# Linear attention between the tiles of a local-attention loop: residual fetched a stage ahead, an empty place behind five of its stages, output in three stages

## The chip, the cores and the metric

The kernel runs on one core of one Trainium2 chip. The time is the device time of one execution in microseconds. The time of a kernel is the median of several executions of the same program; the profile is one further execution, recorded instruction by instruction.

## The reference

Two blocks follow each other over `B = 2` sequences of `N = 2048` tokens with 128 features, all in float32. Each block adds a gated token mixer and a gated local-attention network to the residual `x`:

```python
h = layernorm(x) * (1 + ca) + sa;  x = x + ga * L0_attn(h)     # delta-rule attention
h = layernorm(x) * (1 + cb) + sb;  x = x + gb * L0_ffn(h)      # 6 layers of local attention, 16 heads, window 32
h = layernorm(x) * (1 + ca) + sa;  x = x + ga * L1_attn(h)     # causal linear attention and an MLP
h = layernorm(x) * (1 + cb) + sb;  x = x + gb * L1_ffn(h)      # 2 layers of local attention, 8 heads, window 64
```

The third line is the part that the change touches. Inside, it is

```python
xn = layernorm(x) * ln1_w + ln1_b
Q, K, V = elu(xn @ Wq.T + bq) + 1, elu(xn @ Wk.T + bk) + 1, xn @ Wv.T + bv
attn[t] = Q[t] @ sum_{s<=t} K[s] V[s]^T / (Q[t] . sum_{s<=t} K[s] + 1e-6)
x = x + attn @ Wo.T + bo
x = x + gelu((layernorm(x) * ln2_w + ln2_b) @ F1.T + b1) @ F2.T + b2
```

## The kernel before

After the delta-rule attention (about the first 600 us) all the rest is one long loop in `local_models`. It runs over the 8 layers of the two local-attention networks (6 and 2), over 16 tiles of 128 tokens, and over the 2 sequences: 256 tiles. The loop is a software pipeline. Iteration `i` does, in this order in the program: `scores` of tile i+1 (PE lines L982 and L991, then the softmax on DVE, ACT and POOL), `project` of tile i+3 (L871, in two halves in the 16-head layers), `keys_first_` of tile i (eight transposes, L1026), `values` of tile i+2 (L951, and eight or more copies of `v` by DMA from SyncE), `mix` of tile i (L1043), `turn` of tile i+2 (L923), `turn_out` (L1059) and `project_out` (L1071) of tile i.

Two lists of closures are worked off between these pieces. `steps` holds the six steps of a layer's feed-forward part for a block of 512 tokens (four tiles); `step()` runs one of them at two places of an iteration. `lsteps` holds the stages of the linear attention, and later those of the output; `lstep()` runs one of them, if there is one, at seven places of an iteration:

- place 1: at the top, ahead of `scores`
- place 2: after the first half of `project`
- place 3: after the second half of `project`
- place 4: after `keys_first_` and `values`
- place 5: after `mix` and `turn`
- place 6: after `turn_out`
- place 7: after the second `step()`, ahead of `project_out`

When the last step (`down`) of the sixth layer's feed-forward part is done for a block (b, k), it appends the stages of `linear(b, k)` to `lsteps`. There are 8 such blocks, two every eight iterations. The seventh layer projects its tiles from what these stages write into `hs0`, and calls `lstep()` in a loop if a block is not yet there. When `down` of the last layer is done, it appends `output(b, k)`.

One block of `linear` is a chain with hardly any parallelism: every stage hands on to another engine and gets the result back. `a0` fetches the residual `xb` from `xD` in HBM by DMA (L1247) and adds the gated branch to it on DVE (`outer`, L1187). Then come `centre` (PE L1096, squared on ACT L1098), `variance` (PE L1107, DVE L1112, POOL L1114), `a3` (PE transposes L1120, DVE L1123, ACT L1254 writes `h`), `centre` of `h`, `b2` to `b4` (PE L1263, DVE L1271 to L1282 write `z`, ACT exp), `c1` (PE transposes of `z`, L1291), `c2` to `c4`, `d1` (PE L1357, DVE L1359 writes `h` anew), `centre`, `variance`, `d4`, `e1` (PE L1370, Gelu on ACT), `e2` (PE L1381, DVE L1386 and L1388 write `xb`, which goes back to `xD`, L127), and `centre`, `variance` and `f3` for the next norm. Its buffers (pool `lw`) are single: the next block's `xb` can be fetched only when this block's store and its last `centre` are done.

The order in the program is not quite the order on the chip: the framework's scheduler sorts the instructions by readiness under a model of its own, with the program's order as the priority, and then every engine takes its own queue strictly in the resulting order. PSUM has two buffers of two banks (`wide`) and four of one bank (`bank`), which the loop and the linear stages share.

Of the kernel before, what the change touches and what calls it, by code (L numbers as in the profile page):

```python
# [11 lines left out]
F32 = mybir.dt.float32  # L12
# [8 lines left out]
NBLK = N // 512  # L21
# [51 lines left out]
def tile_kernel(ctx: ExitStack, tc: tile.TileContext, a: dict, out: bass.AP):  # L73
    nc = tc.nc
# [26 lines left out]
    def bc(ap, shape):  # L101
        return ap.to_broadcast(list(shape))
# [16 lines left out]
    xD = dram.tile([128, T], F32, name="xD")  # L119
# [588 lines left out]
    def local_models(mA, mB, hs0):  # L708
# [4 lines left out]
        lw = ctx2.enter_context(tc.tile_pool(name="l_w", bufs=1))  # L713
# [7 lines left out]
        def bank(name):  # L721
            return psT.tile([128, 512], F32, tag="T", name=f"ps_{name}")
# [371 lines left out]
        def centre(S, x, pool, keep):  # L1094
            p = bank("c")
            nc.tensor.matmul(p, lhsT=cen, rhs=x, start=True, stop=True)  # L1096
            S["sq"] = pool.tile([128, 512], F32, name="fsq")
            nc.scalar.activation(S["sq"], p, AF.Square)  # L1098
            if keep:
                S["xc"] = pool.tile([128, 512], F32, tag="t1", name="xc")  # L1100
                nc.scalar.copy(S["xc"], p)

        def variance(S, pool):
            p = bank("var")
            sq = S.pop("sq")
            for j in range(4):
                nc.tensor.matmul(  # L1107
                    p[:, j:j + 1], lhsT=sq[:, j * 128:(j + 1) * 128], rhs=onesm[:, 0:1],
                    start=True, stop=True,
                )  # L1110
            ve = pool.tile([128, 4], F32, name="fve")
            nc.vector.tensor_scalar(ve, p[:, 0:4], 1e-5, None, ALU.add)  # L1112
            S["rt"] = pool.tile([128, 4], F32, name="frt")
            nc.gpsimd.tensor_tensor(S["rt"], ve, bc(nhalf, (128, 4)), ALU.pow)  # L1114
# [11 lines left out]
        def feed_forward(g, b, blk):  # L1126
# [36 lines left out]
            def down():  # L1163
                p = bank("fy")
                for c, sz in enumerate(HSZ):
                    nc.tensor.matmul(  # L1166
                        p, lhsT=wts[g, "w2"][0:sz, c, :], rhs=S[c][0:sz],
                        start=(c == 0), stop=(c == 2),
                    )
                for lo, sh in ((0, 0), (64, 1)):  # L1170
                    cs = slice(n0 + sh, n0 + sh + 512)
                    nc.vector.scalar_tensor_tensor(
                        hs[0][lo:lo + 64, b, cs], p[lo:lo + 64, :], m.vec[lo:lo + 64, l, 8:9],
                        hs[1][lo:lo + 64, b, cs], ALU.add, ALU.add,
                    )
                if l == m.depth - 1:
                    lsteps.extend((linear if m is models[0] else output)(b, blk))
# [5 lines left out]
        def outer(b, k, gate, x):  # L1183

            n0 = k * 512
            for lo, sh in ((0, 0), (64, 1)):
                nc.vector.scalar_tensor_tensor(  # L1187
                    x[lo:lo + 64], hs0[lo:lo + 64, b, n0 + sh:n0 + sh + 512],
                    gate[lo:lo + 64, 5, b:b + 1], x[lo:lo + 64], ALU.mult, ALU.add,
                )  # L1190
# [48 lines left out]
        def linear(b, k):  # L1239
            S = {}  # L1240
            z = K["z"]
            vec = K["vec"]

            def a0():
                x = S["x"] = lw.tile([128, 512], F32, name="xb")
                blk = b * NBLK + k
                nc.sync.dma_start(x, xD[:, blk * 512:(blk + 1) * 512])  # L1247
                outer(b, k, mA, x)

            def a3():  # L1250
                xc = S.pop("xc")
# [140 lines left out]
            def f3():  # L1392
# [9 lines left out]
                ready.add((b, k))  # L1402

            return (
                a0, lambda: centre(S, S["x"], lw, True), lambda: variance(S, lw), a3,
                lambda: centre(S, S["h"], lw, False), b2, b3, b4, c1, c2, c3, c4, d1,
                lambda: centre(S, S["x1"], lw, False), lambda: variance(S, lw), d4, e1, e2,
                lambda: centre(S, S.pop("x"), lw, True), lambda: variance(S, lw), f3,
            )


        def output(b, k):
            S = {}
            blk = b * NBLK + k

            def residual():
                x = S["x"] = lw.tile([128, 512], F32, name="xb")
                nc.sync.dma_start(x, xD[:, blk * 512:(blk + 1) * 512])
                outer(b, k, mB, x)

            def leave():
                p = bank("out")
                x = S.pop("x")
                for c in range(4):
                    nc.tensor.transpose(
                        p[:, c * 128:(c + 1) * 128], x[:, c * 128:(c + 1) * 128], ident
                    )
                o = lw.tile([128, 4, D], F32, tag=f"t{1 + 2 * (k % 2) + b}", name="o")
                nc.scalar.copy(o.rearrange("p c d -> p (c d)"), p)
                nc.sync.dma_start(  # L1430
                    out[blk * 512:(blk + 1) * 512, :].rearrange("(c p) d -> p c d", p=128), o
                )

            return residual, leave


        models[0].consts()
# [9 lines left out]
        for i in range(-3, n):  # L1447
# [7 lines left out]
            if j < n:  # L1455
                g, b, t = tiles[j]
# [47 lines left out]
            if i >= 0:  # L1504
                g, b, t = tiles[i]
# [79 lines left out]
```

## Time and profile before

| | us |
|---|---|
| median of 3 runs | 5089.34 (5084.89 to 5097.49) |
| profiled execution | 5080.23 |
| its span | 5078.4 |
| PE busy | 4669.0 (92%) |
| DVE busy | 3876.9 (76%) |
| ACT busy | 2809.4 (55%) |
| POOL busy | 2760.7 (54%) |

PE is TensorE's matmuls, PEld its weight loads, DVE is VectorE, ACT is ScalarE, POOL is GpSimd, SP is SyncE, which issues the DMAs here. An instruction's idle time is the time that its engine stood still just before it, and the profile names what ended it. The mean granted clock of TensorE over the whole execution was 0.962 of full speed. By the times at which `project_out` of a layer's last tile ends, the fifth layer takes 2862.6 to 3420.6, the sixth 3420.6 to 4188.8, the seventh 4188.8 to 4661.0 us of the span. The linear attention's stages lie between about 3580 and 4360 us, in the sixth layer and at the start of the seventh. The output's stages lie in the last layer.

### The profile page before, as it was taken

The numbers are of one execution on the slowest core, as the hardware profiler recorded it, in microseconds if no ns is written. First come the engines' busy times: TensorE is split into PE (matmuls) and PEld (weight loads), VectorE is DVE, ScalarE is ACT, GpSimd is POOL, SyncE is SP. The second block draws the span as 40 slices with busy tenths as digits, with TensorE's granted clock in tenths as the row PEclk, the third lists the DMA queues.
The fourth block names the chain that finished last, engine by engine and source line by source line (L and its number), as shares of the span: only waits on it lengthen the run. The fifth ranks groups of instructions, "written<-read, shape, count | busy, mean of one in ns | idle before, by whom it ended". The sixth has DMA issues, their size and how long they took to land.

```text
span 5078.4 us, 171451 instructions
## 1 busy us (share of the span) xinstructions
PE 4669.0 (92%) x75012; PEld 3173.1 (62%) x75042; DVE 3876.9 (76%) x6760; ACT 2809.4 (55%) x4649; POOL 2760.7 (54%) x1650
## 2 busy tenths in 40 slices
PE   5657799999999999999999999999999988999998
PEld 4445566666666666666666666666666655566555
DVE  6993488787888788788887787787666656788886
ACT  3323356656656666565665566665555554565554
POOL 3332366566666666566666666666444433455553
PEclk8778899999999999999999999999999999999999
DMA  2000222232222222232222222232111111111121
GB/s 76 1 1 24 84 70 70 59 78 69 64 69 63 77 75 62 62 79 72 63 66 71 72 67 64 64 80 66 49 49 49 48 49 36 40 45 46 51 56 40
DMA packets 222490, 295.63 MB, mean 58 GB/s; under 512 B 75656, under 2 KB 95408, under 8 KB 221744
## 3 DMA queue, kind: packets, MB, share of 16 engines
q1 hardware_dynamic: 221744, 284.67, 21.7%
q8 instruction: 592, 9.70, 0.8%
q14 instruction: 154, 1.26, 0.1%
HBM read 40.98 MB, written 10.75 MB: 10 GB/s over the span
## 4 chain that ended last, share of the span: by engine, by line
PE 75%; DVE 6%; ACT 4%; issue 3%; POOL 2%; DMA 0%; SPq 0%; ACTq 0%; POOLq 0%; DVEq 0%
PE ps_qk L871 15%; PE ps_y L1071 8%; PE ps_turn L923 8%; PE ps_o L1043 7%; PE ps_s L991 7%; PE ps_v L951 6%; PE ps_f L1141 6%; PE ps_oT L1059 4%; PE ps_pT L1026 3%; PE ps_fy L1166 3%; PE ps_c L1096 1%; PE ps_var L1107 1%; PE ps_s L982 1%; ACT sq L873 1%; DVE t L886 1%
## 5 line engine op out<-in xcount | busy, mean ns | idle before, releaser
L892 POOL TENSOR_TENSOR r<-r,t 128x1024 f32<-128x1024 f32 x448 | 1059.6, 2365 | 1151.8 <-DVE t L886 1071.1
L873 ACT ACTIVATE sq<-ps_qk 128x1024 f32<-128x1024 f32 x448 | 459.3, 1025 | 1305.8 <-PE ps_qk L871 1299.7
L904 POOL TENSOR_TENSOR r<-r,rq_y 128x1024 f32<-128x1024 f32 x448 | 844.6, 1903 | 252.1 <-DVE rq_y L180 251.3
L871 PE MATMUL ps_qk<-wp,hs 128*128 128x512 f32 x1792 | 876.4, 611 | 32.8 <-DVE rq_y L180 18.8
L886 DVE TENSOR_TENSOR t<-ps_qk,tb 128x1024 f32<-128x1024 f32 (+1 forms) x512 | 553.4, 1081 | 178.8 <-POOL r L892 178.8
L1017 POOL TENSOR_TENSOR sm<-sm,rs 128x1024 f32<-128x1024 f32 x256 | 489.3, 1912 | 272.8 <-DVE rs L1016 161.4
L881 DVE TENSOR_TENSOR r<-ps_qk,tb 128x1024 f32<-128x1024 f32 (+1 forms) x512 | 548.9, 1072 | 103.3 <-ACT sq L873 101.7
L897 DVE TENSOR_REDUCE ps_qk<-sq 128x16 f32<-128x1024 f32 x448 | 549.7, 1227 | 13.5
L871 PEld LDWEIGHTS ps_qk<-wp,hs 128*128 128x128 f32 x1792 | 310.0, 190 | 351.2 <-issue 257.0
L1071 PEld LDWEIGHTS ps_y<-oT,wo 128*128 128x128 f32 x3584 | 438.5, 192 | 119.0 <-issue 73.4
L1071 PE MATMUL ps_y<-oT,wo 128*128 128x128 f32 x3584 | 481.1, 282 | 17.0 <-ACT oT L1060 16.4
L923 PE MATMUL ps_turn<-ident,r 128*128 128x128 f32 x3584 | 472.5, 282 | 26.0 <-issue 15.5
L1043 PEld LDWEIGHTS ps_o<-v,pT 64*32 64x32 f32 (+1 forms) x26624 | 344.1, 109 | 232.4 <-ACT pT L1027 109.2
L999 DVE TENSOR_REDUCE mx<-ps_s 128x16 f32<-128x1024 f32 (+1 forms) x256 | 313.1, 1223 | 186.7 <-PE ps_s L991 182.5
L951 PE MATMUL ps_v<-wp,hs 128*128 128x512 f32 x896 | 445.8, 597 | 2.1 <-DVE xc L1123 1.6
L923 PEld LDWEIGHTS ps_turn<-ident,r 128*128 128x128 f32 x3584 | 396.3, 143 | 57.8 <-issue 17.7
L1043 PE MATMUL ps_o<-v,pT 64*32 64x64 f32 (+1 forms) x26624 | 392.9, 224 | 37.2 <-issue 19.0
L991 PE MATMUL ps_s<-kT,qT 64*32 64x64 f32 (+1 forms) x26624 | 404.7, 230 | 4.6 <-ACT kT L928 4.1
L991 PEld LDWEIGHTS ps_s<-kT,qT 64*32 64x32 f32 (+1 forms) x26624 | 331.7, 107 | 79.6 <-issue 44.1
L1141 PE MATMUL ps_f<-fx,w 128*128 128x512 f32 (+1 forms) x768 | 364.7, 599 | 1.7 <-DVE fx L1123 1.7
L1049 ACT COPY on<-ps_o 128x512 f32<-128x512 f32 x448 | 244.6, 590 | 215.2 <-PE ps_o L1043 215.0
L1026 PEld LDWEIGHTS ps_pT<-ident,sm 128*128 128x128 f32 x2048 | 244.0, 142 | 145.7 <-issue 142.6
(266 smaller groups left out, 7661.9 us busy)
## 6 DMA issues: line engine op xcount, KB each, us to landing
v<-vn SPq DMA_DIRECT2D x1276, 128.0 KB
v<-vn SPq DMA_DIRECT2D x744, 64.0 KB
v<-vn SPq DMA_DIRECT2D x64, 256.0 KB
wp<-in_L_ffn_Wqkv SPq DMA_DIRECT2D x20, 512.0 KB
xD<-xb SPq DMA_DIRECT2D x24, 256.0 KB
xb<-xD SPq DMA_DIRECT2D x24, 256.0 KB
cs<-in_cos SPq DMA_DIRECT2D x128, 32.0 KB
cs<-in_sin SPq DMA_DIRECT2D x128, 32.0 KB
```

The lines of the kernel that those rows point to most:

```text
L871: nc.tensor.matmul(pq[:, js], lhsT=hw, rhs=wts[g, u][:, js], start=True, stop=True)
L881: nc.vector.tensor_tensor(r[:, es].rearrange("p (h d) -> p h d", d=DH), pq[:, es].rearrange("p (h d) -> p h d", d=DH), bc(tb[:, 0, s].unsq ...
L886: nc.vector.tensor_tensor(t2[:, es].rearrange("p (h s d) -> p h s d", s=2, d=32), pq[:, es].rearrange("p (h s d) -> p h s d", s=2, d=32)[: ...
L892: nc.gpsimd.tensor_tensor(r, r, t2, ALU.add)
L897: nc.vector.tensor_reduce(pq[:, 16 * v:16 * v + 16], st[i].pop(("sq", v)).rearrange("p (h d) -> p h d", d=DH), AX.X, ALU.add,)
L904: nc.gpsimd.tensor_tensor(rv, rv, bc(y[:, 16 * v:16 * v + 16].unsqueeze(2), (128, 16, DH)), ALU.mult)
L923: nc.tensor.transpose(p[:, c * 128:(c + 1) * 128], r[:, cs], ident)
L951: nc.tensor.matmul(p, lhsT=hw, rhs=wv, start=True, stop=True)
L991: nc.tensor.matmul(sp[W * w:W * w + W, c0:c0 + 2 * W], lhsT=qT[64 * q:64 * q + 64, cc, W * w:W * w + W], rhs=kT[64 * q:64 * q + 64, cc, W ...
L1043: nc.tensor.matmul(po[s][W * w:W * w + W, co:co + 64], lhsT=pT[kp, q, c, W * w:W * w + W], rhs=v2[kp, w, co:co + 64], start=True, stop=True,)
L1071: nc.tensor.matmul(py[:, 0:128], lhsT=wts[g, "o"][:, c * NO + s, :], rhs=oT[:, s, c, :], start=(c + s == 0), stop=(c == 3 and s == NO - 1),)
L1141: nc.tensor.matmul(ps_[c][0:sz], lhsT=wts[g, "w1"][:, o:o + sz], rhs=S["x"], start=True, stop=True,)
```

## The change

`linear` gets 27 stages in place of 21. The DMA of the residual leaves `a0` and becomes a stage of its own, `fetch`, with an empty stage between it and `a0`; further empty stages (`rest`, which does nothing) stand behind `a3`, `b4`, `d1` and `e2`. An empty stage takes one of the seven places of an iteration. `output` gets three stages in place of two: `fetch`, `residual`, `leave`. No arithmetic changes, nor do buffers or the number of instructions that compute.

```diff
@@ linear
+            def fetch():
+                blk = b * NBLK + k
+                S["x"] = lw.tile([128, 512], F32, name="xb")
+                nc.sync.dma_start(S["x"], xD[:, blk * 512:(blk + 1) * 512])
+
             def a0():
-                x = S["x"] = lw.tile([128, 512], F32, name="xb")
-                blk = b * NBLK + k
-                nc.sync.dma_start(x, xD[:, blk * 512:(blk + 1) * 512])
-                outer(b, k, mA, x)
+                outer(b, k, mA, S["x"])
+
+            def rest():
+                pass
...
             return (
-                a0, lambda: centre(S, S["x"], lw, True), lambda: variance(S, lw), a3,
-                lambda: centre(S, S["h"], lw, False), b2, b3, b4, c1, c2, c3, c4, d1,
-                lambda: centre(S, S["x1"], lw, False), lambda: variance(S, lw), d4, e1, e2,
-                lambda: centre(S, S.pop("x"), lw, True), lambda: variance(S, lw), f3,
+                fetch, rest, a0, lambda: centre(S, S["x"], lw, True), lambda: variance(S, lw), a3,
+                rest, lambda: centre(S, S["h"], lw, False), b2, b3, b4, rest, c1, c2, c3, c4, d1,
+                rest, lambda: centre(S, S["x1"], lw, False), lambda: variance(S, lw), d4, e1, e2,
+                rest, lambda: centre(S, S.pop("x"), lw, True), lambda: variance(S, lw), f3,
             )
@@ output
+            def fetch():
+                S["x"] = lw.tile([128, 512], F32, name="xb")
+                nc.sync.dma_start(S["x"], xD[:, blk * 512:(blk + 1) * 512])
+
             def residual():
-                x = S["x"] = lw.tile([128, 512], F32, name="xb")
-                nc.sync.dma_start(x, xD[:, blk * 512:(blk + 1) * 512])
-                outer(b, k, mB, x)
+                outer(b, k, mB, S["x"])
...
-            return residual, leave
+            return fetch, residual, leave
```

## The prediction

> **What bounds the kernel now.** I read the page first, then busy time by layer, then PE's waits in the stretch with the linear attention, then the timeline at single waits.
>
> ```profile
> span 5078.4 us, 171451 instructions
> PE 4669.0 (92%) x75012; PEld 3173.1 (62%) x75042; DVE 3876.9 (76%) x6760; ACT 2809.4 (55%) x4649; POOL 2760.7 (54%) x1650
> ```
>
> PE is the bound. The windows of the fifth, sixth and seventh layer (columns: us, busy of PE, PEld, DVE, ACT, POOL, granted clock, DMA share, GB/s):
>
> ```profile
> 2862.60:3420.60 558.00, 547.33 (x10450) 377.27 (x10448) 451.33 (x736) 341.31 (x561) 354.03 (x207) 0.99 0.27 68
> 3420.60:4188.80 768.20, 708.16 (x10850) 475.92 (x10848) 516.77 (x914) 415.84 (x660) 366.06 (x222) 0.96 0.20 52
> 4188.80:4661.00 472.20, 436.99 (x3717) 279.39 (x3716) 354.88 (x757) 258.23 (x407) 223.16 (x145) 0.97 0.15 42
> ```
>
> The fifth layer leaves PE idle for 10.7 us, the sixth for 60, the seventh for 35, and in these two the granted clock is lower. The waits of PE from 3565 to 4340 us (us in total, times, longest):
>
> ```profile
> PE ps_c L1096 <- ACT h L1254: 11.7, 4, 3.3
> PE ps_qk L1291 <- DVE z L1282: 10.1, 6, 3.5
> PE ps_c L1096 <- DVE xb L1388: 5.7, 3, 3.7
> PE ps_c L1096 <- DVE h L1359: 5.1, 4, 2.4
> PE ps_c L1096 <- ACT pT L1027: 4.7, 3, 2.5
> PE ps_r L1120 <- POOL frt L1114: 4.2, 7, 0.9
> ...
> PE ps_c L1096 <- issue: 2.7, 1, 2.7
> ...
> PE ps_c L1096 <- DVE xb L1187: 2.3, 1, 2.3
> ...
> PE ps_c L1096 <- PE ps_s L991: 1.9, 2, 1.0
> ```
>
> Nearly all of PE's idle time here is one linear stage waiting for the one before. The first, second, third and fourth row are the links behind `a3`, `b4`, `e2` and `d1`, where the change puts a rest; the L1096 rows with pT, issue, L1187 and ps_s (11.6 us) are the centre of `xb` behind `a0`. Together 44.2 us.
>
> One such wait in PE's timeline, and windows around it and around another (at 3737.39, 2.35 us idle):
>
> ```profile
> 3601.60 2.08 PE L1096 MATMUL ps_c<-h,cen 128*128 128x512 f32 x2 [3.34 <-ACT h L1254]
> ```
>
> ```profile
> 3593.90:3600.70 6.80, 4.36 (x20) 2.28 (x18) 5.54 (x8) 3.52 (x6) 4.21 (x3) 1.00 0.00 1
> 3600.70:3607.50 6.80, 5.90 (x138) 4.23 (x139) 4.04 (x11) 3.03 (x5) 5.44 (x6) 0.50 0.10 22
> 3737.30:3740.70 3.40, 3.31 (x90) 1.84 (x91) 3.19 (x8) 0.60 (x1) 2.19 (x1) 0.50 0.02 5
> ```
>
> After the wait the clock is 0.50 for 3.4 or 6.8 us: the two matmuls took 2.08 us, where those of ps_c<-hs, after no wait, have a mean of 614 ns each. From 3565 to 4340 us the clock record has 15 such stretches; 11 begin at one of the waits above. Matmul starts within those 11 lie 18.5 us further apart in sum than the medians of the same lines.
>
> **The change part by part.** It adds and removes no computing instruction; it moves stages. What counts is how much other PE work stands between a stage and the next. PE's work per 16-head tile, from the groups' busy time over 256 or 192 tiles: scores 2.35, each half of project 1.96, pT 1.13, values 1.99, mix 1.89, turn 2.11, turn_out 1.11, project_out 2.15. So between places 1 and 2 lie 4.3 us, 2-3 2.0, 3-4 3.1, 4-5 4.0, 5-6 1.1, 6-7 a feed-forward step or nothing, 7-1 2.15. Before, a block has 21 = 3 x 7 stages and always starts at place 7. After, 27 stages: first blocks of a pair start at 7, second blocks at 6. The cover of each link in us:
>
> | link | before | after, first block | after, second block |
> |---|---|---|---|
> | a0 to centre | 2.15 | 2.0 | 4.3 |
> | a3 to centre of h | 3.1 | 1.1 + step | 5.1 |
> | b4 to c1 | 2.15 | 7.1 | 5.1 |
> | d1 to centre | 1.1 | 5.1 | 6.3 |
> | e2 to centre | 3.1 | 6.3 | 6.4 |
>
> The need is the cover before plus the mean wait per block: a0 3.6, a3 4.6, b4 3.4, d1 1.7, e2 3.8. So:
>
> - **d1 and e2**: covered in all blocks. Gain 10.8.
> - **b4**: covered while the tiles are 16-headed. Around the change to the seventh layer they become 8-headed and an iteration takes about 11 us instead of 16.6; in the built order the first block there has only values, mix, turn and turn_out between `b2` and `c1`. The two waits over 3 us before (3.18 and 3.54) belong to blocks around this change; I keep both, 6.7. Gain 3.4.
> - **a3**: second blocks are covered. First blocks get turn_out and, in three of four, three matmuls of the feed-forward gate (L1141, half of 364.7 us over 64 blocks: 2.85). Left: 3.5 once, 0.6 three times: 5.3. Gain 6.4.
> - **a0**: 2.0 in program order is short, but the built order puts `outer` earlier on DVE or the centre behind turn_out in most blocks. I leave 2. Gain 9.6.
>
> Gaps gained: 30.2 us. Of the 11 half-clock stretches (1.7 us each) I leave three, at the three waits over 2.3 us that I leave: gain 13.5.
>
> [...]
>
> **The fetch.** In the built order of both kernels the DMA stands as early as the single `xb` buffer allows. DVE waited for it five times in the kernel, 9.2 us in all, and only 2.3 us of PE's waits name the instruction behind; these are counted at a0. What changes is that blocks now follow each other at once: 54 places of 56 per pair instead of 42. The chain store, landing, fetch, landing took from 3667.87 (end of L1388) to 3675.12 (start of L1187), 7.25 us; from `e2` to `a0` there are now 7 places, a whole iteration of 16.6 or 11 us, so no wait is added. On SP the fetch waits for the store (12.3 us, six times) with the copies of `v` queued behind; those themselves waited 153.5 us for `mix` to free their buffer, so they have room. If that cover went, `mix` would wait: at most 3.3 us a block.
>
> **Output.** PE waited 1.0 us ahead of ps_out (L1425) in each of six blocks before the tail. `leave` moves from behind project_out (place 1) to behind scores and projection (place 2): gain 5 of 6. In the tail the order of instructions is the same.
>
> **New waits.** The stages meet other work: variance to transposes is now often filled with mix and turn while POOL is at its 2.4-us additions; `h2` frees a PSUM bank that turn needs. Nothing in the trace shows them. From below 0; from above see the first rival. The nearest rows are the short waits there now (0.5 to 0.9 us, L1120); I take 1 us a block: 8.
>
> Sum: 30.2 + 13.5 + 5 - 8 = 40.7. From the profiled 5080.2 that is 5039.5; the median of the runs stands 9.1 above the profiled execution, so 5089.3 - 40.7 = 5048.6. I say 5049.
>
> **Rivals.**
> - **Two wide PSUM buffers (slower).** `u`, `kv` and `num` each hold one of two wide buffers until DVE has read them; scores and projection need both. In first blocks `b2` now stands at place 1 and `b3` at 2, with scores and a projection between; in the built order the second half of project slips behind the first matmuls of mix. From the start of `u` to its last read took 4.2 us in the first block before (3609.26 to 3613.48); with a half-clock stretch 5.9. For: PE takes its queue in order. Against: the same tiles cross projections before, and such waits (L871 on DVE sm) came to 3.0 us. It decides when 24 tiles cost over 40.7 + 8 us, 2.0 each; at 3.0 each (72): 5089 - 48.7 + 72 = 5112. Chance 0.12.
> - **Given back (same).** The waits close but the queues of DVE, ACT and POOL, which now carry linear and feed-forward work in every iteration, make the loop wait elsewhere: 4 to 5 us a block, 5 x 8 = 40. For: in the seventh layer DVE is busy 75% beside PE's 93%. Against: in the fifth layer PE is at 98% with DVE at 81%. 5089. Chance 0.14.
> - **The seventh layer takes more of the work and keeps its waits**: gain halved, 5069, still faster. Chance 0.2.
> - The forecast: 0.54.
>
> A measurement of this kernel can tell about 0.3% (15 us) from no change. Faster 0.54 + 0.2 = 0.74, same 0.14, slower 0.12. The low end: every widened wait and its clock gone and no new ones, 44.2 + 18.5 + 5 = 67.7, less the 6.7 around the seventh layer: 5028. The high end takes in the case of no gain: 5092; what lies above is most of the first rival.
>
> **What would show it.** Right: the rows L1096 on h, on xb and on L1359's h, and L1291 on z, fall from 44.2 to some 14 us; the clock of the sixth layer rises from 0.96 to 0.98; the layer gets shorter by some 25 us and the seventh by 10; L1425's idle goes. Wrong: L871 or L982 waiting for z, rq_y or rd (first rival); PE's idle as large as before under other names (second); L1187 waiting for its DMA in all blocks.

## The result, and the profile after

| | before | after |
|---|---|---|
| median, us | 5086.24 (5074.44 to 5097.49, 6 runs) | 5043.47 (5038.07 to 5053.27, 6 runs) |
| ratio | | 0.9923, 95% interval 0.9909 to 0.9937 |
| profiled execution, us | 5080.23 | 5053.27 |

The kernel became faster by 42.8 us, where the prediction had 40.7. The experiments will show that the sum came out so near with a wrong picture of the places behind it, and the terms, measured one by one, do not add up to it. The profiled execution of after is the slowest of its six runs, so the two profiles differ by only 27.0 us.

**A correction comes first.** The text above gives an iteration of the loop seven places for `lstep()`. The printed code has six calls: there is none between `turn_out` and the second `step()`. The places are:

- place 1: at the top, ahead of `scores`
- place 2: after the first half of `project`
- place 3: after the first `step()` and the second half of `project`
- place 4: after `keys_first_` and `values`
- place 5: after `mix` and `turn`
- place 6: after `turn_out` and the second `step()`

This number is used from here on. The prediction's covers, its starting places, and its "54 places of 56" are all wrong. Eight iterations have 48 places. A pair of 21-stage blocks takes 42 of them; a pair of 27-stage blocks takes 54, so each pair slides one iteration further. The traces agree: from the first `ps_c<-xb` of one pair to that of the next took 212.5 us before (3586.3 to 3798.8, eight iterations) and 224.4 us after (3592.4 to 3816.8, nine). And since 27 is 21 plus one whole iteration, blocks start at places 6 and 3 in both kernels.

The page of after:

```profile
span 5051.4 us, 171478 instructions
PE 4682.5 (93%) x75042; PEld 3190.3 (63%) x75042; DVE 3883.5 (77%) x6760; ACT 2796.3 (55%) x4645; POOL 2761.1 (55%) x1650
```

PE is busy no less than before (13.5 us more in the profile); the span shrank because PE stands idle less. The windows of the fifth, sixth and seventh layer of after (columns as before):

```profile
2867.10:3423.10 556.00, 545.53 (x10450) 375.45 (x10448) 451.08 (x736) 340.73 (x561) 353.92 (x207) 1.00 0.27 69
3423.10:4138.40 715.30, 680.39 (x10730) 466.73 (x10728) 514.18 (x885) 400.37 (x645) 363.10 (x218) 0.97 0.21 55
4138.40:4635.10 496.70, 459.61 (x3837) 297.17 (x3836) 365.30 (x786) 263.33 (x418) 227.48 (x149) 0.97 0.15 41
```

The sixth layer is 52.9 us shorter and the seventh 24.5 us longer. PE's idle time fell from 60 to 34.9 us in the sixth and is 37.1 us in the seventh (35.2 before): part of the linear work has slid into the seventh layer, and its waits with it. (These bounds of the layers, here and in the text above, stand one tile late in both kernels. At the true ends, 3403.8, 4163.0 and 4649.4 us before and 3406.4, 4118.8 and 4623.5 after, the sixth layer is 46.8 us shorter and the seventh 18.3 us longer.)

PE's waits in the linear stretch of after (us in total, times, longest), and the groups of the two lines that matter:

```profile
PE ps_r L1120 <- POOL frt L1114: 17.1, 9, 3.6
PE ps_aT L1355 <- DVE at L1347: 6.5, 3, 3.0
PE ps_o L1043 <- ACT pT L1027: 4.9, 5, 2.8
PE ps_qk L1296 <- DVE ps_qk L178: 3.1, 1, 3.1
...
PE ps_qk L1296 <- DVE z L1287: 1.7, 2, 1.3
```

```profile
L1096 PE MATMUL ps_c<-h,cen 128*128 128x512 f32 x30 | 16.3, 626 | 0.0
L1096 PE MATMUL ps_c<-xb,cen 128*128 128x512 f32 x30 | 15.6, 602 | 0.0
L1120 PE MATMUL ps_r<-ident,frt 128*128 128x128 f32 x124 | 20.4, 296 | 17.1 <-POOL frt L1114 17.1
```

Not one row of L1096 is left: the rests closed the links behind `a0`, `a3`, `d1` and `e2` completely. What took part of their place is L1120, the transposes of the reciprocal root of the variance: 4.2 us before, 17.1 now, and 21.6 when the late blocks up to 4480 us are counted too.

### The profile page after: what moved, and what is told of

It reads as the page before. It is cut to its first block, busy times and chain, and to the rows that moved or that the text cites. A ratio compares the mean times of both kernels' runs of the same rounds, so it can differ in the third digit from the quotient of the medians.

```text
span 5051.4 us, 171478 instructions
## 1 busy us (share of the span) xinstructions
PE 4682.5 (93%) x75042; PEld 3190.3 (63%) x75042; DVE 3883.5 (77%) x6760; ACT 2796.3 (55%) x4645; POOL 2761.1 (55%) x1650
## 4 chain that ended last, share of the span: by engine, by line
PE 75%; DVE 6%; ACT 4%; issue 2%; POOL 2%; DMA 0%; SPq 0%; ACTq 0%; POOLq 0%; DVEq 0%
PE ps_qk L871 15%; PE ps_y L1071 8%; PE ps_turn L923 8%; PE ps_o L1043 7%; PE ps_s L991 7%; PE ps_v L951 6%; PE ps_f L1141 6%; PE ps_oT L1059 4%; PE ps_pT L1026 4%; PE ps_fy L1166 3%; PE ps_var L1107 1%; PE ps_c L1096 1%; PE ps_s L982 1%; POOL r L892 1%; ACT sq L873 1%
## 5 line engine op out<-in xcount | busy, mean ns | idle before, releaser
L892 POOL TENSOR_TENSOR r<-r,t 128x1024 f32<-128x1024 f32 x448 | 1059.9, 2366 | 1162.4 <-DVE t L886 1075.2
L886 DVE TENSOR_TENSOR t<-ps_qk,tb 128x1024 f32<-128x1024 f32 (+1 forms) x512 | 552.8, 1080 | 180.5 <-POOL r L892 180.4
L881 DVE TENSOR_TENSOR r<-ps_qk,tb 128x1024 f32<-128x1024 f32 (+1 forms) x512 | 547.7, 1070 | 103.1 <-ACT sq L873 102.1
L897 DVE TENSOR_REDUCE ps_qk<-sq 128x16 f32<-128x1024 f32 x448 | 549.6, 1227 | 13.5
L1071 PE MATMUL ps_y<-oT,wo 128*128 128x128 f32 x3584 | 482.8, 282 | 18.7 <-ACT oT L1060 18.2
L923 PE MATMUL ps_turn<-ident,r 128*128 128x128 f32 x3584 | 470.6, 281 | 22.9 <-issue 12.0
L923 PEld LDWEIGHTS ps_turn<-ident,r 128*128 128x128 f32 x3584 | 395.2, 143 | 54.4 <-issue 15.8
L991 PEld LDWEIGHTS ps_s<-kT,qT 64*32 64x32 f32 (+1 forms) x26624 | 330.1, 107 | 70.3 <-issue 37.3
```

Source lines behind the costliest of these rows:

```text
L881: nc.vector.tensor_tensor(r[:, es].rearrange("p (h d) -> p h d", d=DH), pq[:, es].rearrange("p (h d) -> p h d", d=DH), bc(tb[:, 0, s].unsq ...
L886: nc.vector.tensor_tensor(t2[:, es].rearrange("p (h s d) -> p h s d", s=2, d=32), pq[:, es].rearrange("p (h s d) -> p h s d", s=2, d=32)[: ...
L892: nc.gpsimd.tensor_tensor(r, r, t2, ALU.add)
L897: nc.vector.tensor_reduce(pq[:, 16 * v:16 * v + 16], st[i].pop(("sq", v)).rearrange("p (h d) -> p h d", d=DH), AX.X, ALU.add,)
L923: nc.tensor.transpose(p[:, c * 128:(c + 1) * 128], r[:, cs], ident)
L991: nc.tensor.matmul(sp[W * w:W * w + W, c0:c0 + 2 * W], lhsT=qT[64 * q:64 * q + 64, cc, W * w:W * w + W], rhs=kT[64 * q:64 * q + 64, cc, W ...
```

## The experiments

Each experiment was timed in five rounds against before. For every profile I summed two things in the stretch from 3500 to 4480 us: PE's idle time (gaps over 0.05 us), and the extra time of matmuls under the half clock (start-to-start distances over the medians of the same pairs of lines at full clock). The idle time is sorted by the PE instruction behind it. "Five links" are those behind `a0`, `a3`, `b4`, `d1` and `e2`; "variance" is the wait for `frt`, the reciprocal root, ahead of the transposes (L1120) of `a3`, `d4` and `f3`.

| kernel | stages | idle | of it: five links | variance | half-clock extra | idle + extra, against before | profile from the sixth layer on | median against before |
|---|---|---|---|---|---|---|---|---|
| before | 21 | 84.4 | 50.0 | 4.2 | 31.4 | | | |
| after | 27 | 61.5 | 5.7 | 21.6 | 31.8 | -22.5 | -29.5 | -42.8 |
| e1_rests | 25 | 94.6 | 12.9 | 33.2 | 33.9 | +12.7 | +16.0 | +17.1 |
| e2_fetch | 23 | 96.1 | 13.6 | 44.1 | 36.2 | +16.5 | +16.9 | +20.1 |
| e3_output | 21 | 83.8 | 50.0 | 4.3 | 32.6 | +0.6 | -2.2 | 0.0 |
| e4_lump | 27 | 71.6 | 23.6 | 13.7 | 11.6 | -32.6 | -32.5 | -32.8 |
| e5_rests_dve | 25 | 102.1 | 13.8 | 41.1 | 23.4 | +9.7 | +13.5 | +19.1 |
| e6_after_dve | 27 | 68.7 | 17.8 | 13.2 | 18.7 | -28.4 | -31.4 | -28.8 |
| e7_lump7 | 28 | 78.0 | 19.1 | 15.2 | 36.6 | -1.2 | +2.1 | -0.1 |
| e8_rest_var | 27 | 54.2 | 6.2 | 6.8 | 31.3 | -30.3 | -32.6 | -32.0 |
| e9_var_at_3 | 27 | 79.9 | 7.6 | 30.7 | 36.9 | +1.0 | +4.1 | +1.6 |
| e10_best27 | 27 | 81.5 | 19.8 | 12.5 | 43.3 | +9.0 | +10.2 | -1.4 |
| e11_33stages | 33 | 66.5 | 12.7 | 9.2 | 37.3 | -12.0 | -15.3 | -19.0 |
| e12_second_later | 21, second blocks 27 | 82.8 | 30.5 | 18.9 | 42.9 | +9.9 | +9.1 | +8.6 |

Idle time and half-clock time together account for the profiled difference to within 4 us in every experiment (7 us in after). So the profiles are read from these two. The medians need not differ by as much as single profiles do: after gains 29.5 us by its profile and 42.8 by the medians.

### The parts of the change one at a time

**e1_rests**: the four rests alone, with 25 stages; fetch and output as before.

```diff
-a0, centre, variance, a3, centre, b2, b3, b4, c1, ... d1, centre, ... e2, centre, variance, f3
+a0, centre, variance, a3, rest, centre, b2, b3, b4, rest, c1, ... d1, rest, centre, ... e2, rest, centre, variance, f3
```

> Only the four empty stages behind a3, b4, d1 and e2 are added (25 stages); the residual is fetched in a0 and the output has two stages, as before. Theory 1 (the gain comes from the closed waits between two linear stages on PE): most of the gain is here, 20 to 35 us, and the waits of L1096 on h and on L1388's xb and of L1291 on z fall by more than half; the centre behind a0 keeps some of its 11.6 us. Theory 2 (the earlier fetch brings the gain): no change. Theory 3 (the gain comes from linear work that slides into the seventh layer, whose PE has more free time, 7% against 2%): four of six added places, so two thirds of the gain, some 28 us, with the waits unchanged.

**e2_fetch**: the stages `fetch` and the first `rest` alone, 23 stages.

```diff
-a0, centre, variance, a3, ...
+fetch, rest, a0, centre, variance, a3, ...
```

> Only the residual's fetch is a stage of its own with one empty stage behind it (23 stages); no other empty stage, output as before. Theory 1: a3 to centre of h now has 1.1 us of cover in first blocks and 2.15 in second ones against a need of 4.6, so what a0 gains is lost there: from 8 us faster to 8 us slower. Theory 2: the whole gain, some 40 us. Theory 3: two of six places, 14 us faster.

**e3_output**: only `output` in three stages; `linear` as before.

> Only the output has three stages; linear as before. Theory 1 as predicted: the six idle times of 1.0 us ahead of ps_out go, 5 us faster; by the profile after, where the last layer got only 1 us shorter, 0 to 2 us, which these runs can't tell from none. Theories 2 and 3: no change.

**e4_lump**: the 21 stages unbroken, with the six empty places in a lump behind `f3`.

```diff
-..., centre, variance, f3
+..., centre, variance, f3, rest, rest, rest, rest, rest, rest
```

> Linear keeps its 21 stages in unbroken order, and six empty stages stand behind f3 (27 in all, as many as after the change); residual fetched in a0, output as before. The same delay and the same slide into the seventh layer, without any spacing. Theory 1: no gain, rather 5 to 20 us slower, since second blocks now start at place 6, where a0 to centre, and b4 to c1, have no matmuls between them. Theory 3: the whole gain, some 40 us faster. Theory 2: no change.

Measured: e1_rests 5098.27, ratio 1.0031 (1.0019 to 1.0043); e2_fetch 5101.24, ratio 1.0041 (1.0028 to 1.0054); e3_output 5081.19, ratio 1.0000 (0.9989 to 1.0011); e4_lump 5048.36, ratio 0.9934 (0.9919 to 0.9949); before 5081.18.

So two parts of the change, each alone, make the kernel slower, and a version that spaces nothing gains 33 us. Neither the rests nor the early fetch brings the gain alone, and a gain of this size needs no spacing. Theory 3 (sliding) had the gain of e4_lump about right, but had 28 us for e1_rests and 14 for e2_fetch. The waits of e1_rests, e2_fetch and e4_lump, one row each:

```profile
PE ps_r L1120 <- POOL frt L1114: 32.7, 14, 5.9
```

```profile
PE ps_r L1120 <- POOL frt L1114: 44.1, 18, 6.0
```

```profile
PE ps_r L1120 <- POOL frt L1114: 13.6, 9, 4.7
```

The rests of e1_rests do close their links (50.0 to 12.9 us in the table), but the wait for `frt` takes back 29.0 us and other waits 18.3 us. What makes that wait is seen in the timeline of e2_fetch, in its second block:

```profile
3684.58 1.02 PE L1096 MATMUL ps_c<-xb,cen 128*128 128x512 f32 x2
3687.29 1.05 PE L1107 MATMUL ps_var<-onesm,fsq 128*128 128x1 f32 x8
3688.11 1.21 DVE L886 TENSOR_TENSOR t<-ps_qk,tb 128x1024 f32<-128x1024 f32 x1
...
3689.11 1.88 PE L951 MATMUL ps_v<-wp,hs 128*128 128x512 f32 x4
3689.24 0.24 DVE L1016 RECIPROCAL rs<-rs 128x16 f32<-128x16 f32 x1
3689.40 1.16 DVE L881 TENSOR_TENSOR r<-ps_qk,tb 128x1024 f32<-128x1024 f32 x1
3689.47 2.35 POOL L892 TENSOR_TENSOR r<-r,t 128x1024 f32<-128x1024 f32 x1 [6.43 <-DVE t L886]
...
3691.78 1.90 POOL L1017 TENSOR_TENSOR sm<-sm,rs 128x1024 f32<-128x1024 f32 x1
3691.85 1.22 DVE L886 TENSOR_TENSOR t<-ps_qk,tb 128x1024 f32<-128x1024 f32 x1 [1.29 <-POOL r L892]
3692.99 0.15 DVE L1112 TENSOR_SCALAR fve<-ps_var 128x4 f32<-128x4 f32 x1
...
3693.64 2.34 POOL L892 TENSOR_TENSOR r<-r,t 128x1024 f32<-128x1024 f32 x1
3695.94 1.01 POOL L1114 TENSOR_TENSOR frt<-fve,nhalf 128x4 f32<-128x4 f32 x1
...
3697.01 1.12 PE L1120 MATMUL ps_r<-ident,frt 128*128 128x128 f32 x4 [6.02 <-POOL frt L1114]
```

The variance matmuls end at 3688.3. Their consumer on DVE takes 0.15 us, but it stands behind the rotary products of the projection just done and starts at 3692.99; one of those (L886) waits 1.29 us for POOL's L892. The `pow` on POOL takes 1.0 us, but stands behind another 2.34 us of L892. PE has only `keys_first_` and `values` to do meanwhile and then stands still for 6.02 us. This is a variance at place 3, right behind the projection. In e2_fetch second blocks start at place 5, which puts the variance of `x` and that of `x1` at place 3: 6.0, 6.0, 4.2, 3.1 and 3.5, 3.6, 1.5, 2.8 us in the four blocks, 30.7 of its 44.1. Before and after have no variance at place 3.

e3_output shows that the third stage gains nothing. PE's waits in the last layer, first of before, then of e3_output:

```profile
PE ps_o L1043 <- ACT pT L1027: 6.1, 11, 0.7
PE ps_out L1425 <- issue: 3.0, 3, 1.0
PE ps_out L1425 <- DVE xb L1187: 2.1, 2, 1.0
```

```profile
PE ps_o L1043 <- ACT pT L1027: 8.1, 11, 1.7
PE ps_v L951 <- ACT o L1431: 3.7, 3, 1.2
```

The 5.1 us ahead of `ps_out` are gone, and 5.7 us stand in their place: `values` waits until ACT has copied `ps_out` out of PSUM, and `mix` waits longer for `pT`.

### POOL, or the place?

The next four tell apart whether POOL's `pow` is what costs, and what a number of stages does by itself. Their theories C and D still reckon with seven places.

**e5_rests_dve** and **e6_after_dve**: e1_rests and the changed kernel, with the reciprocal root of `linear`'s variances on DVE:

```diff
-nc.vector.tensor_scalar(ve, p[:, 0:4], 1e-5, None, ALU.add)
-nc.gpsimd.tensor_tensor(S["rt"], ve, bc(nhalf, (128, 4)), ALU.pow)
+nc.vector.tensor_scalar(xm, p[:, 0:4], 1e-5, None, ALU.add)
+... # nine more DVE instructions of 128x4: seed and polynomial of the reciprocal root
```

> The four rests alone (25 stages, as in e1_rests), with one thing changed: the four variances of the linear block compute their reciprocal root by nine small instructions on DVE in place of POOL's pow. Theory A (POOL's queue: the rests close their links, but the stages then meet POOL's 2.4 us additions, and pow stands behind them): PE's wait for frt falls from 32.7 us to under 10, and the time falls from 5098 by about that much, to 5065-5080. Theory B (where the blocks stand in the loop decides, and the wait for frt is only one face of it): the wait moves to DVE with about its size, and the time stays at 5090-5105. Bound of the added work: 8 x 4 x 9 instructions of about 0.1 us, 29 us of DVE, which is 77% busy.

> The changed kernel, with the four variances of the linear block on DVE in the same way. Theory A: PE's wait for frt, 17.1 us in the changed kernel, falls to some 5, and the time falls from 5043 to 5030-5036. Theory B: 5040-5050, with new waits for DVE.

**e7_lump7**: e4_lump with seven empty places, 28 stages.

> The block unbroken in 21 stages, with seven empty places behind its last one: 28, so that every block starts at the same place (7) as before the change and meets the same work of attention in the same order; only the idle iteration between pairs is shared out between the blocks. Theory C (spreading: the gain of e4_lump comes from blocks no longer standing two at a time and then none, so that the feed-forward steps run beside linear stages): 5045-5055. Theory D (places: the gain comes from second blocks starting one place earlier, at 6): no gain, 5075-5090, with waits at the same links as before (44 us). Theory A alone says little: the wait for frt stays near 4-14.

**e8_rest_var**: 27 stages, the empty places elsewhere.

```diff
-fetch, rest, a0, centre, variance, a3, rest, ... b4, rest, ... d1, rest, centre, variance, d4, e1, e2, rest, centre, variance, f3
+fetch, a0, centre, variance, rest, a3, rest, ... b4, rest, ... d1, centre, variance, rest, d4, e1, e2, centre, variance, rest, f3
```

> 27 stages and the output in three as in the changed kernel, but the empty places stand elsewhere: behind the three variances of x, x1 and the last x (where PE waits for POOL's pow), behind the second and the ninth stage (a3 and b4) and none behind the fetch, d1 or e2. Theory A: PE's wait for frt falls from 17.1 us to under 6; the links behind a0, d1 and e2 are open again (31 us before the change, of which e4_lump with 27 stages showed some 20); time 5035-5050. Theory B or D (27 stages alone decide): 5043-5050, whatever the waits are.

Measured: e5_rests_dve 5100.89, ratio 1.0037 (1.0025 to 1.0050); e6_after_dve 5053.03, ratio 0.9944 (0.9925 to 0.9962); e7_lump7 5081.71, ratio 0.9994 (0.9982 to 1.0006); e8_rest_var 5049.81, ratio 0.9941 (0.9919 to 0.9962); before 5081.80.

Theory A falls. The row of e5_rests_dve that answers to 32.7 us of e1_rests:

```profile
PE ps_r L1145 <- DVE frt L1139: 37.9, 10, 8.3
```

Taken off POOL, the wait is there under DVE's name and no smaller. The run does not weigh the two engines against each other, though, since nine more small instructions now take their turns on DVE (0.15 to 0.18 us each in the timeline from 3692.4 us on, but for L1137 with 1.81). In the longest wait (8.3 us, which ends at 3604.1) those from L1130 to L1139 lie between 3597.1 and 3604.1, with four instructions of 1.2 us (L881, L886 and twice L897) in between. What it shows is that leaving POOL in this way does not help. In e6_after_dve the wait for `frt` is 13.2 us in place of 21.6, but the five links cost 17.8 in place of 5.7, and its time, 5053.0, lies above what either theory expected.

e7_lump7 and e4_lump differ by one empty place. With 28 stages, four more than a multiple of six, the starting places turn (6, 4, 2, 6, ...), and nothing is gained: spreading (theory C) is not enough by itself. With 27, blocks start at 6 and 3 as before, and 33 us are gained. Theory D had the right time here for a wrong reason, since second blocks of e4_lump do not start earlier. In e8_rest_var the rests stand behind the variances, the wait for `frt` falls to 6.6 us (under 6 was expected), and PE's idle is the lowest of all, 54.2 us:

```profile
PE ps_r L1120 <- POOL frt L1114: 6.6, 6, 2.3
PE ps_aT L1355 <- DVE at L1347: 5.8, 3, 2.9
```

The links behind `a0`, `d1` and `e2`, which have no rest in it, cost 0.5 us and not the 20 to 31 that I expected. The extra stages ahead of them moved them to other places, and there they were covered.

### The place, tested

Only for these four were the places counted as six.

**e9_var_at_3**: e8_rest_var with two rests moved by one stage, everything else in its place.

```diff
-fetch, a0, centre, variance, rest, a3, rest, centre, ... variance, rest, d4, e1, ...
+fetch, a0, centre, variance, a3, rest, rest, centre, ... variance, d4, rest, e1, ...
```

> An iteration of the loop has six places. e8_rest_var with two empty places moved by one stage: from behind the variances of x and x1 to behind a3 and d4, so that these follow the variance at once; every other stage keeps its place. In first blocks the variance of x stands at place 3 (behind the projection), in second blocks that of x1. Theory P (place: behind the projection the variance's small instruction stands behind five or six DVE instructions of 1.2 us and pow behind a 2.3 us addition on POOL, and only keys and values, 3.1 us, cover it): PE waits for frt 6.0 us at a3 in first blocks and 3.5 at d4 in second blocks, as in e1_rests and e2_fetch where a variance stood there; four of each with the last ones shorter, 25 to 38 us more idle, so 5075-5088. Rival N (only the number of stages decides: 27 is good, 25 and 23 are not): 5045-5053.

**e10_best27**: the rests where the waits of the runs so far, sorted by link and place, sum to the least.

```diff
+fetch, a0, rest, centre, variance, rest, a3, rest, centre, b2, ... d1, centre, variance, rest, d4, e1, e2, rest, centre, variance, f3
```

> 27 stages with the empty places where the waits measured so far, sorted by link and place, sum to the least: behind a0, the variance of x, a3, the variance of x1 and e2, and none behind b4, d1 or the other variances; output in three. Theory P: PE idle in the linear stretch falls from 61.5 us in the changed kernel (54.2 in e8_rest_var) to 45-52, time 5030-5045. Rival N: 5043-5050. Above 5055: the table by places does not carry over to the end of the sixth and the seventh layer, where iterations are shorter.

**e11_33stages**: a rest at eleven links.

```diff
+fetch, a0, centre, rest, variance, rest, a3, rest, centre, b2, b3, b4, c1, rest, c2, c3, rest, c4, d1, rest, centre, variance, rest, d4, e1, rest, e2, rest, centre, rest, variance, rest, f3
```

> 33 stages, which start at the same places (6 and 3) as 21 and 27, with an empty place at eleven links. Theory P: nearly no wait at a link while tiles have 16 heads; but each pair takes 11 iterations, so three of the eight blocks run in the seventh layer, whose shorter iterations cover less. 5025-5050 if the links there hold with two places each; 5050-5075 if that layer's waits grow. Rival N says nothing of 33.

**e12_second_later**: the unbroken block, six rests ahead of second blocks only.

```diff
-return (
+return (rest,) * (6 * b) + (
```

> The unbroken block of 21 stages, with six empty places ahead of every second block only: 21 + 27 = 48 places, exactly the eight iterations between pairs. Every stage has the place it had before (first blocks start at 6, second at 3), first blocks stand in the same iteration, second blocks one iteration later; nothing moves on into the seventh layer. Theory O (in e4_lump the second blocks came to stand beside feed-forward steps, which cover them): PE idle of second blocks falls from 8-12 us to 3-7 each, time 5048-5065. Theory M (e4_lump gained because the work slides on by five iterations): no gain, 5078-5088.

Measured: e9_var_at_3 5088.05, ratio 1.0007 (0.9997 to 1.0017); e10_best27 5084.99, ratio 0.9997 (0.9988 to 1.0005); e11_33stages 5067.44, ratio 0.9959 (0.9947 to 0.9971); e12_second_later 5095.01, ratio 1.0014 (1.0006 to 1.0022); before 5086.43.

e9_var_at_3 decides for the place. In both versions the variance of `x` in first blocks and that of `x1` in second blocks stand at place 3; in e8_rest_var a rest follows, in e9_var_at_3 the transposes follow at once. With the same number of stages and these two rests moved by one stage, all of e8_rest_var's gain is gone:

```profile
PE ps_r L1120 <- POOL frt L1114: 28.8, 13, 5.4
```

The wait for `frt` grew by 22.2 us and all of PE's idle by 25.7, the least that was expected; single waits were shorter than in e2_fetch (5.4, 1.9, 3.3 and 4.2 us at `a3` of first blocks where I had 6.0). Rival N, that 27 stages are good by themselves, falls.

e10_best27 missed: 5030 to 5045 expected, nothing gained. Its idle is 81.5 us, with 15.8 at the link behind `b4` (4.4, 5.9 and 3.0 in the last three blocks, in and around the seventh layer) and 34.7 outside the linear stages (22.6 in after). The table by places does not carry over; that it was made from iterations with 16 heads and from other orders of instructions is a likely reason, but no run shows it. e11_33stages gains 19.0 us, less than half of what after does: the five links and the variances still cost 21.9 us, and PE's idle outside the linear stages is 32.2 us.

e12_second_later gives every stage its old place and its old iteration, except that second blocks come one iteration later. It is slower by 8.6 us: theory O falls, and so does the idea that second blocks gain by standing beside feed-forward steps. Theory M had expected no gain, and misses by 7 us. Its wait for `frt` is 18.9 us against 4.2 before, though no variance stands at place 3 and every stage has its old place: 14.8 us of it lie at `a3` of the four second blocks. In the longest (5.0 us, which ends at 3929.4) the variance's DVE instruction stands behind L841, which itself waits 2.5 us for POOL's L856. These two lines belong to `tables`, which the loop calls in every second iteration only. So the place alone does not settle a wait; what else the iteration holds counts too. Nor is it enough that the work slides on by one iteration per pair, in which e4_lump differs from e12_second_later: e9_var_at_3 and e10_best27, with 27 stages, slide as far and gain nothing.

No version was measured to be faster than the changed kernel. e4_lump, e8_rest_var and e6_after_dve (0.9934, 0.9941 and 0.9944 against 0.9923) have intervals that overlap with its own.

### What stays open

e4_lump gains 32.8 us, of which 12.8 are less idle and 19.8 less half clock. e12_second_later has the same first two blocks (7.4 and 6.5 us of waits in both) and yet 105.5 us at half clock in the stretch, where e4_lump has 27.3. The windows from 3500 to 4480 us of before, after, e4_lump and e12_second_later, of which the number after the busy times is the clock:

```profile
3500.00:4480.00 980.00, 895.48 (x11612) 592.29 (x11604) 659.77 (x1248) 522.60 (x821) 441.68 (x274) 0.96 0.18 47
```

```profile
3500.00:4480.00 980.00, 918.19 (x11895) 619.61 (x11894) 689.11 (x1297) 528.67 (x845) 457.08 (x284) 0.96 0.18 48
```

```profile
3500.00:4480.00 980.00, 908.22 (x11939) 604.70 (x11940) 691.26 (x1311) 541.55 (x855) 460.74 (x285) 0.99 0.19 49
```

```profile
3500.00:4480.00 980.00, 897.13 (x11537) 603.94 (x11535) 651.93 (x1236) 507.81 (x809) 437.64 (x274) 0.95 0.18 47
```

The last section counts PE's idle time in the windows of a fixed grid: all 197 windows with over 2.0 us of it were followed by the half clock. In this stretch, e4_lump has 5 such windows, e12_second_later 11 and before 12. Of windows with 1.6 to 2.0 us, e4_lump has 6, of which 1 was followed by the half clock, and e12_second_later 8, of which 6 were. Why the waits of e4_lump fall so favourably on the grid is not settled; it does not depend on one lucky profile, since all six of its times lie between 5035.52 and 5061.46, with a mean clock of 0.963 to 0.969.

## Why the prediction was right or wrong

- **The bound**: right. PE is busy 4682.5 us after and 4669.0 before; what moved is its idle time.
- **The places**: wrong. Six, not seven. The table of covers and "first blocks at 7, second blocks at 6" fall with it, and so does the claim that every block fits its eight iterations. Counted with six, each of the five links gets about two intervals where it had one, except that behind `a0`, which gets `turn_out` or half a projection and a step; it had no wait either.
- **The widened links**: right in kind, somewhat low. From 3500 to 4480 us they fell from 50.0 us to 5.7, by 44.3 where I had 30.2; I left 14. What is left is at `b4`, 3.1 and 2.2 us in late blocks and 0.4 in an early one, where I had kept 6.7. For `a0` and `a3` I left 7.3 and nothing was left.
- **The half clock**: wrong as far as the profile shows. I counted 13.5 us; the extra went from 31.4 to 31.8 in the profiled execution. The waits that remained drew as much of the slow clock. The other five runs are faster than the profiled one by 6 to 15 us, with a mean clock of 0.961 to 0.965 against its 0.959, so part of that gain may be there; no profile shows it.
- **The fetch**: right that nothing is gained by the DMA itself. DVE's waits for it fell from 9.2 us to 3.0:

```profile
DVE xb L1187 <- DMA xb<-xD: 3.0, 2, 1.8
```

- **Output**: 5 us expected, none in e3_output. The step that failed is that nothing was looked for behind `ps_out` in the same PSUM.
- **New waits**: the term that was far too small. I took 8 us from short waits of 0.5 to 0.9 us at L1120. The widened links gave 44.3 us over the whole stretch and PE's idle fell by 22.9, so 21.4 us came back: 17.4 at the variances, 1.6 outside the linear stages, the rest at other links. The reason given, POOL's 2.4 us additions, was half of it: in e2_fetch's timeline 4.7 us pass in DVE's queue and 2.8 in POOL's before the two small instructions start.
- **The seventh layer**: I had both layers shorter, by 25 and 10 us; by the same bounds they changed by -52.9 and +24.5, since the work slides by one iteration per pair.
- **The first rival** (two wide PSUM buffers) did not come: none of the waits that it named is over 2 us in the stretch. **The second** (given back) is what e1_rests, e2_fetch, e7_lump7 and e9_var_at_3 show: links closed, time unchanged or worse. It was given 0.14, and is the outcome of most arrangements tried; that the changed kernel is not among them was not in my reasons.

So the time was right, and in part by luck. Two terms (links 14.1 us too small, new waits 13.4 too small) nearly cancel, while the 13.5 us of half clock and the 5 us of the output did not come. Measured in this way the sum is some 22.5 us and not 40.7; the rest of the 42.8 us between the medians is not traced to any term. And the mechanism "rests cover links" holds for the links alone, not for the kernel.

## What to carry to other kernels

A stage that is added to a list worked off at fixed places moves every stage behind it: count the calls in the source, work out the place of each stage before and after, and cost every link, not only the ones that are widened. A tiny instruction costs what stands ahead of it in its queue; behind a projection, in e2_fetch, that was 6.02 us of PE's time for 0.15 us of work on DVE and 1.01 us on POOL. And a part of a change may be worse than nothing alone and good beside another part, so "which line brings the gain" can have no answer.

## What the runs showed of the hardware

In these runs PE's waits were followed by the half clock the more often the longer they were, from 37 of 1056 to 72 of 83. In nine of the profiles (before, after, e1_rests, e2_fetch and e4_lump to e8_rest_var), counted from 1000 us on, a stretch at 0.50 began during a wait or within 3.6 us of its end for:

| PE's wait, us | followed by half clock |
|---|---|
| 0.3 to 1.0 | 37 of 1056 |
| 1.0 to 1.5 | 35 of 203 |
| 1.5 to 2.0 | 27 of 66 |
| 2.0 to 2.6 | 67 of 116 |
| over 2.6 | 72 of 83 |

The clock records show more than odds. In each of the 14 profiles, all stretches at 0.50 after 1000 us (25 in before, 26 in after) begin and end on a fixed grid of 3.413 us, within 2 ns (the end of the last stretch is left out). I summed PE's idle time in every window of that grid that ran at full clock, up to 20 us before the end:

| PE's idle in the window, us | next window at half clock |
|---|---|
| under 1.6 | 60 of 15820 |
| 1.6 to 2.0 | 85 of 140 |
| over 2.0 | 197 of 197 |

So here the idle time inside one window tells more than the length of one wait: 197 of 197 over 2.0 us were followed by the half clock, beside 72 of the 83 waits over 2.6 us in nine profiles. In before, the wait of 2.35 us that ends at 3737.4 lies with 2.24 us in one window and is followed by the half clock, while one of 3.34 us from 3810.8 on is cut by the grid into 1.61 and 1.73 us and is not. The 60 windows with less idle time are not explained, and no trace shows what sets the grid.
